# Two-layer graph network, 16 graphs: the turning of the first norm's output moves from TensorE to VectorE and DRAM

## The chip, the cores and the metric

The kernel runs on one core of one Trainium2 chip. What counts is the device time of one execution in microseconds (us), the median of the runs. A profiled execution gives a page of figures and a trace; its times are counted from its first instruction to its last (the span). Engines: PE is TensorE (matmuls), DVE is VectorE, ACT is ScalarE, POOL is GpSimd, and SP only issues transfers.

## The reference

The input is x, 16 graphs of 1024 nodes with 256 channels, and one matrix adj of 1024x1024. Everything is float32.

```python
# layer 0
h = jnp.maximum(_layernorm(x, axis=-1), 0.0)
c = mean of h over the channels                 # one number for each node
A = |sigmoid(c_m - c_n) - 0.5| ...              # weights from the differences
g = relu(einsum('bcn,bnm->bcm', h^T, adj * A_s) * para)   # becomes the queries q
k, v = split(h @ kv_w)
out = softmax(q k^T * scale) v                  # 4 heads of 64 channels
x = x + out
# layer 1
h = jnp.maximum(_layernorm(x, axis=-1), 0.0)
agg = A_hat @ h                                 # A_hat: adj + 1, normed by degrees
y = agg @ W1.T + b1;  batchnorm over all nodes of all graphs;  relu
z = h1 @ W2.T + b2;   batchnorm over all nodes of all graphs
x = x + z
```

The products `h @ kv_w` contract over the channels. A matmul on TensorE contracts over the partitions, so h, which lies with nodes in the partitions, must be turned: `ht` has channels in the partitions and nodes in the row. This turning is what the change concerns. Attention sums over all keys, so the order of the keys is free, as long as k and v have the same order.

## The kernel before

A graph's x lies as 8 tiles of 128 nodes, `[128, 8, 256]`. For each graph b the kernel makes: the first norm's output `h_a`; the weighed matrix tiles `w` (ScalarE: `Abs`, then `Tanh`; VectorE: times `adj`); the queries `q` (products `pg`); `ht`; keys and values (products `pk` and `pv`, from `ht`); attention; the second norm's output `h_b`; the aggregation (products `pa`, with tiles `aht` of the graph matrix kept in DRAM); and the hidden layer (products `py`, results `y` written to DRAM by POOL). When all graphs are through, a second part reads `y` back and ends the work.

The order is written out by hand. `attention()` walks through 16 steps for each graph: two score tiles `sc` (TensorE), their exponentials `p` (ScalarE, four buffers), the additions `acc` (VectorE), the products with the values `o` of the step before. Beside the attention of graph b, a generator `background(b)` supplies the other work in pieces: the remaining products for graph b+1 (keys, queries, values), the aggregation of graph b-1, and `prepare(b + 2, ...)` with the hidden products of graph b-1. Every piece has a cost (1.71 for a product) and the loop takes pieces until a share of `total` is reached, about three products in each step. A piece that yields `TOP` asks that the next piece stand behind the scores at the top of the next step.

`prepare(b, products)` issues one hidden product, three more with three slots of the weighing `w`, then the turning of one half of the channels at the top of a step, again products with weighing, the turning of the other half, and the rest. `transposed(b, k)` does the turning: for each of two halves of the nodes four TensorE transposes of 128x128 into one PSUM bank (`htp`, line 396), and one ScalarE copy of 128x512 from the bank to `ht` (line 399). The banks of all these products come from one pool, `ps_mm`, with two buffers, so a product can start only when the one two before it has been copied out.

Other pools that matter: tag `h` (two buffers, for `h_a` and `h_b`), tag `ht` (three buffers, shared by `ht` and the aggregation's result `at`), tag `adj` (three buffers). SP's queue holds the loads of `adj`, `para`, `aht` and `x` in the order in which they are issued; a load that must wait holds those behind it. POOL's queue holds the small steps of the norms and the writes of `y`, of x and, in graph 0, the work on the graph matrix (`graph()`).

Of the kernel before, what the change touches and what calls it, by code (L numbers as in the profile page):

```python
# [10 lines left out]
F32 = mybir.dt.float32  # L11
# [6 lines left out]
P = 128  # L18
# [5 lines left out]
def gnn_two_layers_kernel(  # L24
# [12 lines left out]
    nc = tc.nc  # L37
    B, N, C = x.shape
    H1 = w1_t.shape[1]
    NT = N // P  # L40
    CC = C // P
# [11 lines left out]
    dram = ctx.enter_context(tc.tile_pool(name="dram", bufs=1, space=DRAM))  # L53
# [15 lines left out]
    aht_d = dram.tile([7, NP // 2, P, TH, FB], F32, name="aht_d")  # L69
    y1_d = [dram.tile([P, HC, FB], F32, name=f"y1_d{i}") for i in range(B * NH)]  # L70

    csum_d = [dram.tile([N], F32, name=f"csum_d{b}") for b in range(B)]
    dinv_d = dram.tile([N], F32, name="dinv_d")

# [5 lines left out]
    SQ = 32  # L80
    NS = P // SQ
# [14 lines left out]
    def layers(shifted):  # L96
# [10 lines left out]
        p2 = st.enter_context(tc.tile_pool(name=f"p2_{kind}", bufs=2))  # L107
        p3 = st.enter_context(tc.tile_pool(name=f"p3_{kind}", bufs=3))
# [11 lines left out]
        xs, hs, hts, ats, qs, ks, vs = {}, {}, {}, {}, {}, {}, {}  # L120
        invs = {}
        csums, cbcs, weighted, weighers = {}, {}, {}, {}
# [9 lines left out]
        def advance(pieces):  # L132

            due = queue[:]
            queue.clear()
            cost = next(pieces, None)
            for action in due:
                action()
            return cost

        def run(*parts):
            for part in parts:
                while advance(part) is not None:
                    pass
            while queue:
                queue.pop(0)()

        def weave(main, *sides):

            for i, cost in enumerate(main):  # L150
                for start, side in sides:
                    if i >= start:
                        cost += next(side, 0.0)
                yield cost
            for _, side in sides:
                yield from side
# [7 lines left out]
        def bank(name):  # L164
            return ps_mm.tile([P, FB], F32, tag="mm", name=name)
# [217 lines left out]
        TOP = -1.0  # L383

        def transposed(b, k, halves=range(NH)):

            h = hs["a", b]
            if 0 in halves:
                ht = p3.tile([P, N], F32, tag="ht", name=f"ht_{b}_{k}")
                hts.setdefault(b, []).append(ht)  # L390
            ht = hts[b][k]
            for g in halves:
                pt = bank(f"htp_{b}_{k}_{g}")
                for j in range(FB // P):
                    t = g * (FB // P) + j
                    nc.tensor.transpose(
                        pt[:, j * P : (j + 1) * P], h[:, t, k * P : (k + 1) * P], ident
                    )
                nc.scalar.copy(ht[:, g * FB : (g + 1) * FB], pt)  # L399

        def differences(b):

            cbc = p1.tile([P, N], F32, tag="cbc", name=f"cbc_{b}")
            cbcs[b] = (
                cbc.rearrange("p (t q) -> p t q", t=NT)
                if b <= 1
                else cbc.rearrange("p (q t) -> p t q", t=NT)
            )  # L410
            weighers[b] = weigh(b)
            if b == 0:
                broadcast_row(cbc, columns_of(csums[b], f"c{b}"), f"c{b}")
                return
            if b == 1:
                turned = bank(f"csumt_{b}")[0:NT, 0:P]
                nc.tensor.transpose(turned, csums[b], ident)
                row = p1.tile([P, NT // 2, P], F32, tag="s1", name=f"csumr_{b}")[0:NT, 0, :]
                nc.scalar.copy(row, turned)
                nc.sync.dma_start(out=csum_d[b].rearrange("(t p) -> t p", p=P), in_=row)  # L420
            else:
                nc.sync.dma_start(out=csum_d[b].rearrange("(p t) -> p t", p=P), in_=csums[b])
            nc.sync.dma_start(
                out=cbc, in_=csum_d[b].rearrange("(o n) -> o n", o=1).to_broadcast([P, N])
            )
# [43 lines left out]
        AHEAD = 6  # L469
# [310 lines left out]
        def prepare(b, products):  # L780


            yield from islice(products, 1)
            w = weighers[b]
            for k in range(CC):
                yield from weave(islice(products, 3), (0, islice(w, AHEAD // 2)))
                yield TOP
                transposed(b, k)
                yield 1.0
            yield from products  # L790

        endings, turns = [], []
# [89 lines left out]
        def scores(b, k, f, g):  # L882


            made = []
            for m in (2 * g, 2 * g + 1):
                sc = ps_sc.tile([P, 2, FB], F32, tag="sc", name=f"sc_{b}_{k}_{f}_{m}")
                for e in range(2):
                    r = slice(e * HD, (e + 1) * HD)
                    nc.tensor.matmul(  # L890
                        sc[:, e, :],
                        ks[b][k][r, m * P : (m + 1) * P],
                        qs[b][k][r, f * FB : (f + 1) * FB],
                        start=True,
                        stop=True,
                    )
                pr = p4.tile([P, 2, FB], F32, tag="p", name=f"p_{b}_{k}_{f}_{m}")
                nc.scalar.activation(pr, sc, AF.Exp)  # L898
                made.append(pr)
            return made  # L900
# [107 lines left out]
        def attention():  # L1008

            units = [Unit(b, k, f) for b in range(B) for k in range(CC) for f in range(NH)]  # L1010
            steps = [(u, g) for u in units for g in range(NG)]
            per_graph = CC * NH * NG
            before = None
            at_top, at_end, adds = {}, {}, {}
            bg, done, total, top = iter(()), 0.0, 0.0, False
            for s in range(len(steps) + 2):
                if s < len(steps):
                    unit, g = steps[s]
                    b = unit.at[0]
                    if s % per_graph == 0:  # L1020
                        run(bg)
                        top = False
                        bg, done = background(b), 0.0
                        total = (37.6 if b > 0 else 41.0) * (b + 1 < B) + 24.0 * (b > 0) + 6.0 * (b + 2 < B)
                        total += 13.7 * (0 < b < B - 2) + 27.4 * (b == B - 1) + 3.0 * (b == 0)

                        total -= 10.3 * (b == B - 1)
                    made = scores(*unit.at, g)
                    due = total * (s % per_graph + 1) / per_graph
                else:  # L1030
                    due += 5.1
                for action in at_top.pop(s, ()):
                    action()
                if top:
                    done += advance(bg)
                    top = False
                if s in adds:
                    adds.pop(s)()
                if s < len(steps):
                    for pr in made:  # L1040
                        unit.add(pr)
                if before is not None:
                    (last, g_last), prs = before
                    last.values(g_last, prs)
                    if g_last == NG - 1:

                        one = (0, 0, 1, 1) if last.index == UNITS - 1 else (0, 1, 3, 4)
                        for e in range(2):
                            at_end.setdefault(s + one[e], []).append(lambda u=last, e=e: u.fold(e))
                        at_top.setdefault(s + one[2], []).append(last.sums)  # L1050
                        at_top.setdefault(s + one[3], []).append(last.finish)
                        adds[s + one[3]] = last.add_output
                while done < due and not top:
                    cost = advance(bg)
                    if cost is None:
                        break
                    if cost == TOP:
                        top = True
                        break
                    done += cost  # L1060
                for action in at_end.pop(s, ()):
                    action()
                before = (steps[s], made) if s < len(steps) else None
            run(bg)

        with st:
# [22 lines left out]
            else:  # L1089
# [10 lines left out]
                products = keys_values(0)  # L1100
# [9 lines left out]
                load_x(2)  # L1110
                run(weave(plain_queries(0), (0, weighers[0]), (5, Norm(1, True).all())))
                attention()
                attn.close()
                turns.append(second(kind))
# [325 lines left out]
```

## Time and profile before

| | us |
|---|---|
| median of 3 runs | 2608.92 |
| lowest and highest run | 2606.27, 2610.16 |
| span of the profiled execution (time around it is not listed) | 2604.3 |
| PE busy | 2525.9 |
| DVE busy | 1822.7 |
| ACT busy | 1460.7 |
| POOL busy | 391.3 |
| PE L396, `htp`, 256 transposes, busy (they overlap) | 36.5 |
| ACT L399, copies to `ht`, 64 | 34.6 |

Busy time of an engine says how long instructions ran on it, not that the kernel waited for it. The chain of work that ended last says for each moment of the span what the end waited for. In the timeline a row is a run of equal instructions: start, length, engine, line, operation, output from inputs, count, and in brackets the idle time before with what ended it. Matmuls overlap, so the distance between starts says more than the lengths.

### The profile page before, as it was taken

The numbers are of one execution on the slowest core, as the hardware profiler recorded it, in microseconds if no ns is written. First come the engines' busy times: TensorE is split into PE (matmuls) and PEld (weight loads), VectorE is DVE, ScalarE is ACT, GpSimd is POOL, SyncE is SP. The second block draws the span as 40 slices with busy tenths as digits, with TensorE's granted clock in tenths as the row PEclk, the third lists the DMA queues.
The fourth block names the chain that finished last, engine by engine and source line by source line (L and its number), as shares of the span: only waits on it lengthen the run. The fifth ranks groups of instructions, "written<-read, shape, count | busy, mean of one in ns | idle before, by whom it ended". The sixth has DMA issues, their size and how long they took to land.

```text
span 2604.3 us, 31375 instructions
## 1 busy us (share of the span) xinstructions
PE 2525.9 (97%) x11627; PEld 931.8 (36%) x11627; DVE 1822.7 (70%) x2837; ACT 1460.7 (56%) x2034; POOL 391.3 (15%) x456
## 2 busy tenths in 40 slices
PE   7999999999999999999999999999999999999994
PEld 3333333333333333333333333333333333334443
DVE  4768686867767686868677676858686776657774
ACT  6774565647474746656464747465564634335543
POOL 1540001000101000010001010000100001036653
PEclk9999999999999999999999999999999999999997
DMA  3654224152524343241525243433315242355459
GB/s 138 229 171 173 93 99 154 54 189 73 182 83 152 111 148 101 102 150 55 183 71 182 86 156 107 147 100 114 137 62 180 66 166 105 109 196 221 170 198 367
DMA packets 130915, 363.46 MB, mean 140 GB/s; under 512 B 15288, under 2 KB 32192, under 8 KB 124608
## 3 DMA queue, kind: packets, MB, share of 16 engines
q1 hardware_dynamic: 110144, 282.70, 31.3%
q0 software_dynamic: 20608, 78.66, 7.9%
q8 instruction: 94, 1.54, 0.2%
q14 instruction: 69, 0.57, 0.1%
HBM read 286.79 MB, written 74.51 MB: 139 GB/s over the span
## 4 chain that ended last, share of the span: by engine, by line
PE 87%; ACT 7%; DMA 2%; issue 2%; DVE 1%; SPq 0%; POOL 0%; POOLq 0%; DVEq 0%; ACTq 0%
PE sc L890 17%; PE o L931 16%; PE pa L171 15%; PE pg L171 14%; PE py L171 8%; PE m_f L1235 7%; PE pk L171 4%; PE pv L171 4%; ACT w L458 3%; DMA out_dram<-xo_f 2%; ACT p L898 2%; PE ot L986 1%; ACT w L466 1%; PE sums L961 1%; ACT ht L399 1%
## 5 line engine op out<-in xcount | busy, mean ns | idle before, releaser
L898 ACT ACTIVATE p<-sc 128x1024 f32<-128x1024 f32 x512 | 495.0, 1020 | 452.5 <-PE sc L890 452.1
L920 DVE TENSOR_TENSOR acc<-acc,p 128x1024 f32<-128x1024 f32 x384 | 472.2, 1230 | 143.2 <-ACT p L898 121.8
L890 PE MATMUL sc<-q,k 64*128 64x512 f32 x2048 | 509.0, 615 | 4.7 <-ACT p L898 4.6
L931 PE MATMUL o<-p,v 128*64 128x512 f32 x2048 | 495.9, 605 | 0.0
L171 PE MATMUL pg<-w,h_a 128*64 128x512 f32 x1600 | 357.9, 592 | 3.1 <-DVE q L612 2.3
L171 PE MATMUL pa<-aht,h_b 128*64 128x512 f32 x1536 | 344.0, 592 | 3.5 <-ACT h_b L341 3.4
L890 PEld LDWEIGHTS sc<-q,k 64*128 64x128 f32 x2048 | 175.9, 186 | 325.5 <-issue 284.4
L458 ACT ACTIVATE w<-cbc,csum 128x512 f32<-128x512 f32 x256 | 285.5, 1168 | 0.0
L171 PE MATMUL py<-at,w 128*64 128x512 f32 x1024 | 232.8, 597 | 8.4 <-ACT ht L399 7.0
L445 DVE SCALAR_TENSOR_TENSOR w<-w,adj 128x1024 f32<-128x1024 f32 x128 | 157.5, 1230 | 114.8 <-ACT w L466 110.8
L931 PEld LDWEIGHTS o<-p,v 128*64 128x64 f32 x2048 | 124.1, 136 | 250.3 <-issue 247.2
L171 PEld LDWEIGHTS pg<-w,h_a 128*64 128x64 f32 x1600 | 114.7, 137 | 232.0 <-issue 214.4
L746 POOL DMA_DIRECT2D y_d<-y x128 | 70.5, 551 | 795.0 <-ACT y L745 787.2
L171 PEld LDWEIGHTS pa<-aht,h_b 128*64 128x64 f32 x1536 | 110.8, 137 | 216.9 <-issue 208.3
L745 ACT ACTIVATE y<-py,vec 128x512 f32<-128x512 f32 x128 | 87.6, 684 | 142.3 <-PE py L171 119.7
L749 DVE BATCH_NORM_STATS2 stats<-y 128x6 f32<-128x512 f32 x128 | 85.7, 687 | 79.6 <-ACT y L745 79.5
L466 ACT ACTIVATE w<-w 128x1024 f32<-128x1024 f32 x128 | 135.2, 1056 | 1.7
L520 DVE TENSOR_TENSOR w<-w,w 128x1024 f32<-128x1024 f32 x112 | 132.8, 1217 | 1.5
L341 ACT ACTIVATE h_b<-x,lnsm_b 128x256 f32<-128x256 f32 x128 | 70.4, 609 | 110.7 <-DVE lnsm_b L330 110.7
L93 POOL TENSOR_SCALAR lnsm_b<-mv_b 128x4 f32<-128x4 f32 x32 | 12.1, 379 | 791.5 <-DVE mv_b L319 791.4
L171 PEld LDWEIGHTS py<-at,w 128*64 128x64 f32 x1024 | 72.2, 137 | 162.4 <-issue 129.8
L171 PE MATMUL pk<-ht,kvw_f 128*64 128x512 f32 x512 | 117.0, 599 | 1.5 <-ACT ht L399 1.5
(158 smaller groups left out, 2779.7 us busy)
## 6 DMA issues: line engine op xcount, KB each, us to landing
aht<-aht_d SPq DMA_DIRECT2D x224, 512.0 KB, 6.3
adj<-in_adj_dram SPq DMA_DIRECT2D x128, 512.0 KB, 4.4
y_d<-y POOLq DMA_DIRECT2D x128, 256.0 KB, 2.6
yin_f<-y_d SPq DMA_DIRECT2D x32, 1024.0 KB, 6.3
x<-in_x_dram SPq DMA_DIRECT2D x32, 512.0 KB, 5.1
para<-in_para_dram SPq DMA_DIRECT2D x64, 256.0 KB, 3.9
x_d<-x POOLq DMA_DIRECT2D x16, 1024.0 KB, 10.3
xo_f<-x_d SPq DMA_DIRECT2D x32, 512.0 KB, 8.6
```

Of the source, the lines that this page charges most:

```text
L171: nc.tensor.matmul(dst[r], left[:, r], right, start=start, stop=stop)
L445: nc.vector.scalar_tensor_tensor(w, w, 1.0, a, op0=ALU.add, op1=ALU.mult)
L458: nc.scalar.activation(w[:, t, :].rearrange("p (t q) -> p t q", q=P), cbc[:, q * NT // NH : (q + 1) * NT // NH], AF.Abs, bias=csum[:, th * ...
L466: nc.scalar.activation(made[i], made[i], AF.Tanh, scale=-0.5 / C)
L520: nc.vector.tensor_sub(block(i)[part], block(x)[part], block(y)[part])
L745: nc.scalar.activation(y, made, AF.Identity, bias=b1[:, j : j + 1])
L749: nc.vector.bn_stats(stats1[:, j, i, :], y)
L890: nc.tensor.matmul(sc[:, e, :], ks[b][k][r, m * P : (m + 1) * P], qs[b][k][r, f * FB : (f + 1) * FB], start=True, stop=True,)
L898: nc.scalar.activation(pr, sc, AF.Exp)
L920: nc.vector.tensor_add(self.acc, self.acc, pr)
L931: nc.tensor.matmul(self.o[r, :], vs[b][k][:, m, r], pr[:, e, :], start=(m == 0), stop=(m == NT - 1),)
L1235: nc.tensor.matmul(made, left[:, j, :], right[:, j, :], start=(j == 0), stop=(j == JH - 1))
```

## The change

From graph 2 on (`prepare` serves graphs 2 to 15; graphs 0 and 1 are still turned by TensorE) `transposed` is replaced by two functions. `squares(b)` lets VectorE transpose each square of 32x32 in place of the whole, for both halves of the channels, into a third tile of tag `h`, and POOL writes this tile, 1 MB, to a new DRAM tensor `hsq_d`. `gathered(b, k)` lets SP read it back into `ht`, in four transfers for each half of the channels: each fills 32 partitions with 4 runs of 256 elements from 4 groups of partitions. So the squares reach their places between partitions, and the nodes in `ht` stand in another order than before, the same for keys and values. In `prepare` the pieces are arranged anew: `squares` after the first hidden product, `gathered(b, 0)` after the fourth, `gathered(b, 1)` after the fifth; no piece asks for the top of a step. The cost of the turning in `total` becomes 4.0 for 6.0.

```diff
+    hsq_d = [dram.tile([P, CC, N], F32, name=f"hsq_d{b}") for b in range(B)]
...
+        def squares(b):
+            sq = p2.tile([P, CC, N], F32, tag="h", name=f"sq_{b}")
+            for k in range(CC):
+                nc.vector.transpose(
+                    sq[:, k].rearrange("p (i t s) -> p i t s", i=NS, s=SQ),
+                    hs["a", b][:, :, k * P : (k + 1) * P].rearrange("p t (i s) -> p i t s", s=SQ),
+                )
+            nc.gpsimd.dma_start(out=hsq_d[b], in_=sq)
+
+        def gathered(b, k):
+            ht = p3.tile([P, N], F32, tag="ht", name=f"ht_{b}_{k}")
+            hts.setdefault(b, []).append(ht)
+            src = hsq_d[b][:, k].rearrange("(j s) (i r) -> i s j r", s=SQ, i=NS)
+            for i in range(NS):
+                nc.sync.dma_start(
+                    out=ht[i * SQ : (i + 1) * SQ].rearrange("s (j r) -> s j r", j=NS), in_=src[i]
+                )
...
         def prepare(b, products):
+            w = weighers[b]
             yield from islice(products, 1)
-            w = weighers[b]
-            for k in range(CC):
-                yield from weave(islice(products, 3), (0, islice(w, AHEAD // 2)))
-                yield TOP
-                transposed(b, k)
-                yield 1.0
+            squares(b)
+            yield from weave(islice(products, 3), (0, islice(w, AHEAD // 2)))
+            gathered(b, 0)
+            yield from weave(islice(products, 1), (0, islice(w, 1)))
+            gathered(b, 1)
+            yield from weave(islice(products, 2), (0, islice(w, AHEAD // 2 - 1)))
             yield from products
...
-                        total = (37.6 if b > 0 else 41.0) * (b + 1 < B) + 24.0 * (b > 0) + 6.0 * (b + 2 < B)
+                        total = (37.6 if b > 0 else 41.0) * (b + 1 < B) + 24.0 * (b > 0) + 4.0 * (b + 2 < B)
```

## The prediction

> **What bounds the kernel now.** I read the page first (busy shares, then the chain of work that ended last), and then the timeline of TensorE around one set of the transposes that the change removes.
>
> ```profile
> PE 2525.9 (97%) x11627; PEld 931.8 (36%) x11627; DVE 1822.7 (70%) x2837; ACT 1460.7 (56%) x2034; POOL 391.3 (15%) x456
> ...
> PE 87%; ACT 7%; DMA 2%; issue 2%; DVE 1%; SPq 0%; POOL 0%; POOLq 0%; DVEq 0%; ACTq 0%
> ```
>
> TensorE is busy 97% of the span and holds 87% of the chain; VectorE, at 70%, holds 1%. So TensorE's order is the clock of the middle part. The pieces of the chain confirm it: the first product `pk` of a graph starts at these times.
>
> ```profile
> 321.76 5.15 PE pk L171 x24
> ...
> 464.61 5.15 PE pk L171 x24
> ...
> 607.46 5.15 PE pk L171 x24
> ```
>
> The distance is 142.85 us each time. A graph that takes exactly as long as the last one is set by one engine that doesn't wait for varying things. Hence time taken from TensorE inside such a period should come off the span, unless something new is late.
>
> Now the transposes of graph 5 (`htp`), in the timeline of TensorE (start, length, operation, count, idle time before):
>
> ```profile
> 724.49 1.94 PE L931 MATMUL o<-p,v 128*64 128x512 f32 x8
> 726.26 1.89 PE L171 MATMUL py<-at,w 128*64 128x512 f32 x8
> 728.08 1.99 PE L890 MATMUL sc<-q,k 64*128 64x512 f32 x8
> 729.99 1.09 PE L396 MATMUL htp<-ident,h_a 128*128 128x128 f32 x8
> 731.02 1.94 PE L931 MATMUL o<-p,v 128*64 128x512 f32 x8
> 733.50 5.37 PE L171 MATMUL py<-at,w 128*64 128x512 f32 x24 [0.54 <-ACT ht L399]
> 738.80 1.99 PE L890 MATMUL sc<-q,k 64*128 64x512 f32 x8
> 740.72 0.41 PE L961 MATMUL sums<-part,same 128*128 128x32 f32 x2
> 740.96 1.07 PE L396 MATMUL htp<-ident,h_a 128*128 128x128 f32 x8
> 741.96 1.94 PE L931 MATMUL o<-p,v 128*64 128x512 f32 x8
> 744.00 1.94 PE L171 MATMUL py<-at,w 128*64 128x512 f32 x8
> ```
>
> Read start to start, since matmuls overlap. The two groups of 8 take 1.03 and 1.00 us. After `o`, the next product normally starts 1.77 us later (724.49 to 726.26); after the first group it starts 2.48 us later and after the second 2.04 us, so 0.71 and 0.27 us more. That is `py` waiting for one of two PSUM banks until ScalarE has copied `htp` out (L399).
>
> [...] the fold's 128x512 transpose takes 699 ns and an ordinary 128x512 addition about 690. [...] SP waits for POOL's write; the trace has such waits (SP for `x_d`, 13 times, 117.8 us in all, 9.9 at most).
>
> **The change part by part.**
>
> Removed, for each of 14 graphs (2 to 15): 16 transposes, 2.03 us of TensorE, and the two late starts, 0.98 us. Sum 3.0 us; I take 2.95, since `sums` then has the slightly longer step to `o` seen elsewhere (0.33 for 0.24 us). Four ScalarE copies (2.4 us) also go; I count them at nothing, because ScalarE is idle 44% of the time.
>
> Added on VectorE: two transposes of 128x1024. By the 699 ns for half that width, and by the 1.23 us of other 128x1024 operations (about 1.15 start to start), some 2.4 us. Lower bound 2.3; upper bound, if runs of 32 elements cost double, 4.8. They stand behind the last addition and scaling of the aggregation, so at that point nothing new is waited for. Queued behind them are the statistics of `y`, the fold and the next `acc` additions, which free `p` for ScalarE. In 700 to 760 us VectorE has gaps of 1 to 4 us at every step, and the four `p` buffers leave about a step of 8.9 us. Taken at nothing; if that cover were gone, 2.4 us a graph.
>
> Added on POOL: one write of 1 MB, about 0.63 us of issue and 10.3 us to landing, by the `x_d` write of the same size (transfers to and from `x_d`: 3.9 to 13.7). Only the small `y_d` writes stand behind it: the second waits one issue longer, and its `y` buffer is wanted again four products later.
>
> Added on SP: 8 gathers of 128 KB in runs of 1 KB. SP needs about 0.45 us for an issue, so 3.6 us. Runs of 1 KB are known from the load of `x`: 512 KB land in 5.1 us. Two of these in a row, 10.2 us, bound 1 MB from above; 5.1 + 3.6 = 8.7 is what I take. Behind the gathers in SP's queue is the fourth load of `adj`, wanted only in the next graph (before, its use is at 756, some 25 us after it could be issued).
>
> **Is the trip hidden?** In the built program's order the hidden products `py` move together: two in one step of attention, three in each of the next two, and the last step has none. From the start of the first `py`, by the trace's distances (`sc` 1.92, `o` 1.77, a product 1.75, `ot` 0.59, `sums` 0.33 us): 3.5 + 8.94 + 8.94 + 4.02 + 4.28 = 29.7 us until the next graph's `pk`, which needs `ht`. The chain: final addition and scaling 1.4, transposes 2.4, write 10.3, gathers 8.7: 22.8 us. Spare, 6.9 us; with the slow ends (13.7 and 10.2) still 2. The transfer engines stand nearly still after 707 us, so no crowd is to be expected. Price when hidden: nothing.
>
> The empty step leaves ScalarE 4.0 us of TensorE time for two exponentials (first end 1.18 + 0.97 us after `sc` starts, second 3.1). Working through ScalarE's new order, the weighing before it ends in time by about 0.3 to 1 us. So no stall, but this is the thinnest place.
>
> Graph 0 is different (period 178.75 minus its start, with ScalarE and POOL as the limits). POOL's queue has the writing of the graph matrix and the `deg` power in front of the new write, and reaches them only at 164 to 167 us. Then a write of about 7 (10.3 was in a crowd of loads; bounds 5 and 10.3) and 8.7: `ht` of graph 2 lands near 183 where `pk` started at 178.75. That is a loss of about 4 us, bounds 0 and 8; the transposes' 2 us there were inside a ScalarE wait anyway (2.43 and 1.92 us of idle TensorE).
>
> **Sum.** 13 x 2.95 = 38.4 saved, 4 lost: 34.4 us. The profiled execution's span of 2604.3 becomes 2570; the page lists no time around the span, and the runs' median, 2608.92, stands 4.6 above it. So 2574.5.
>
> **Rivals.**
>
> A, the trip is late (ends slower). `pk` waits for the gathers, and as TensorE works in order everything behind it waits too. Each gather writes only 32 of 128 partitions, a shape that the trace before doesn't show. The point from which it decides: the trip longer than 29.7 us by more than the saving of 2.95, that is a write and gathers of about 29 us from issue to landing where I have 19. If eight gathers went at half the rate of `x` (20.4 us) behind a write of 13.7, the trip is 1.4 + 2.4 + 13.7 + 0.6 + 20.4 = 38.5, late by 8.8, net +5.9 in each of 13 graphs and some 16 in graph 0: about 2701. For it: the unknown shape. Against it: 16 transfer engines idle in that stretch, the spare 7 us. Chance 0.12.
>
> B, the saving is halved by a new wait. ScalarE or VectorE is late in the empty step (weighing, statistics and the transposes stand closer together), and `sc` waits for `p`; 1.5 us a graph: 38.4 - 19.5 - 4 = 15 us, 2594. For it: the waits of 2.43 and 1.92 us in graph 0, where weighing stood before an attention-only step. Against it: in the later graphs ScalarE waited only 0.3 us or more for work at these places and loses 2.4 us of copies. Chance 0.13.
>
> C, nothing moves: the freed TensorE time is all taken back as waits, or the transposes are overlapped by weight loads more than start-to-start shows. Against it: the 97% and the constant period. Chance 0.03.
>
> **How the numbers follow.** Main case 0.72: 2574.5, its own range 2566 (no loss in graph 0, 14 x 3.0 saved) to 2583. B reaches 2600. The range 2564 to 2600 takes in the main case and B with their bounds on the unknown costs and leaves A out, 0.12, and C, 0.03. Faster by over 0.2% (5.2 us, about what a measurement of this kernel can tell from no change): main case and B, 0.85; within: C, 0.03; slower: A, 0.12.
>
> **What would show it.** Right: no `htp` after graph 1; the first `pk` of neighbouring graphs 139.9 us apart; VectorE transposes of 128x1024 at 1.2 us; gathers landing several us ahead of `pk`; the waits of `py` for `ht` gone. Wrong: `pk` waiting for a DMA in each graph (A); `sc` waiting for `p` in the last step of a graph (B); transposes much above 1.2 us; a period that stays at 142.85 (C).

## The result, and the profile after

| | before | after |
|---|---|---|
| median, us | 2609.27 | 2572.42 |
| lowest and highest of 4 runs, us | 2606.27, 2610.16 | 2571.51, 2573.06 |
| span of the profiled execution, us | 2604.3 | 2570.6 |

The ratio is 0.986 (95% interval 0.9847 to 0.9872): faster by 36.9 us in the medians. The profiled execution after took 2572.44 us, 1.8 us more than its span, so its span stands for the median. The span of before does not: of the 29 executions of that kernel on record 7 took 2605.84 to 2606.69 us and 22 took 2608.5 to 2610.43, none lies between, and the profiled one, with a span of 2604.3, belongs to the 7.

The busy shares of the page after, to be held against those of before:

```profile
PE 2497.0 (97%) x11403; PEld 913.0 (36%) x11403; DVE 1851.1 (72%) x2865; ACT 1432.0 (56%) x1978; POOL 396.8 (15%) x470
```

TensorE has 224 matmuls and 28.9 us less. VectorE has 28.4 us more, ScalarE 28.7 us less, and TensorE is still the only engine near its limit.

The groups of instructions (line, engine, operation, output and inputs, shapes, count; busy time, mean ns of one; idle time of the engine before them and what ended it). First two lines: the transposes on TensorE and on VectorE. Third: the product that used to wait for ScalarE's copies. Last: the same product in the kernel before.

```profile
L397 PE MATMUL htp<-ident,h_a 128*128 128x128 f32 x32 | 6.2, 323 | 9.0 <-ACT h_a L342 8.5
...
L408 DVE STREAM_TRANSPOSE sq<-h_a 128x1024 f32<-128x1024 f32 x28 | 33.1, 1219 | 0.0
...
L172 PE MATMUL py<-at,w 128*64 128x512 f32 x1024 | 230.7, 598 | 0.0
...
L171 PE MATMUL py<-at,w 128*64 128x512 f32 x1024 | 232.8, 597 | 8.4 <-ACT ht L399 7.0
```

`htp` is left for two graphs only. The idle time in front of `py`, 8.4 us before, is 0.0.

The timeline of TensorE at the same place as before, the end of graph 5's preparation:

```profile
715.91 1.94 PE L955 MATMUL o<-p,v 128*64 128x512 f32 x8
717.68 5.32 PE L172 MATMUL py<-at,w 128*64 128x512 f32 x24
722.93 1.99 PE L914 MATMUL sc<-q,k 64*128 64x512 f32 x8
724.85 1.94 PE L955 MATMUL o<-p,v 128*64 128x512 f32 x8
726.62 5.32 PE L172 MATMUL py<-at,w 128*64 128x512 f32 x24
731.87 1.99 PE L914 MATMUL sc<-q,k 64*128 64x512 f32 x8
...
740.26 5.32 PE L172 MATMUL pk<-ht,kvw_f 128*64 128x512 f32 x24
...
1998.79 5.32 PE L172 MATMUL pk<-ht,kvw_f 128*64 128x512 f32 x24
```

No row here has a bracket: TensorE waits for nothing. Every `o` to `py` is the ordinary 1.77 us. This `pk` and the one of the last graph, nine graphs later, are 1258.53 us apart (740.26 to 1998.79), so the period is 139.84 us, 3.01 less than before. The kernel before had its `pk` for graph 2 and for the last graph at these times:

```profile
178.75 5.32 PE L171 MATMUL pk<-ht,kvw_f 128*64 128x512 f32 x24
...
2035.77 5.32 PE L171 MATMUL pk<-ht,kvw_f 128*64 128x512 f32 x24
```

The changed kernel starts the first of them at 180.91, 2.2 us later, and the last 37.0 us earlier. Thirteen periods lie between the two: 13 x 3.01 = 39.1 us saved, 2.2 lost in graph 0.

The trip that replaces the transposes, from the timelines of VectorE, POOL and SP:

```profile
712.02 2.36 DVE L408 STREAM_TRANSPOSE sq<-h_a 128x1024 f32<-128x1024 f32 x2
```
```profile
714.68 0.54 POOL L412 DMA_DIRECT2D hsq_d<-sq  x1 [0.66 <-DVE sq L408]
```
```profile
718.97 4.21 SPq L420 DMA_DIRECT2D ht<-hsq_d  x8
```

The write is issued at 714.68 and SP's gathers follow at 718.97, 4.3 us later. The eight issues end at 723.18; with a median of 4.0 us from issue to landing (2.4 to 6.3 over all 112 gathers) the last one is there at about 727. `pk` needs it at 740.26: some 13 us to spare.

### The profile page after: what moved, and what is told of

Its sections match the earlier page's. It is cut to its first block, busy times and chain, and to the rows that moved or that the text cites. A ratio compares the mean times of both kernels' runs of the same rounds, so it can differ in the third digit from the quotient of the medians.

```text
span 2570.6 us, 31151 instructions
## 1 busy us (share of the span) xinstructions
PE 2497.0 (97%) x11403; PEld 913.0 (36%) x11403; DVE 1851.1 (72%) x2865; ACT 1432.0 (56%) x1978; POOL 396.8 (15%) x470
## 3 DMA queue, kind: packets, MB, share of 16 engines
q1 hardware_dynamic: 126272, 297.39, 33.7%
## 5 line engine op out<-in xcount | busy, mean ns | idle before, releaser
L172 PE MATMUL pk<-ht,kvw_f 128*64 128x512 f32 x512 | 117.9, 603 | 1.5 <-ACT ht L400 1.5
L172 PE MATMUL pv<-kvw_f,ht 128*64 128x256 f32 x1024 | 115.9, 379 | 0.0
## 6 DMA issues: line engine op xcount, KB each, us to landing
x_d<-x POOLq DMA_DIRECT2D x16, 1024.0 KB, 10.3
```

The source lines that it names most:

```text
L172: nc.tensor.matmul(dst[r], left[:, r], right, start=start, stop=stop)
```

## The experiments

The theory: the transposes' TensorE time and the late starts behind them are the saving; the trip through DRAM is hidden; 2.2 us were lost in graph 0; and between the two profiled executions another 3.3 us were lost in the end part. The main rival is that the new arrangement of `prepare`, not the turning, moved the time. All ratios are to the kernel before on the same chip.

### The arrangement alone

```diff
-            squares(b)
...
-            gathered(b, 0)
+            transposed(b, 0)
...
-            gathered(b, 1)
+            transposed(b, 1)
```

> The change's arrangement of the hidden products and its smaller total are kept, but the turning is done by TensorE as before (16 transposes and 4 ScalarE copies a graph, at the places of the gathers, not at the top of a step). Theory (the saving is TensorE's own time, 2.03 us of transposes and 0.98 us of waiting for PSUM banks a graph): the period returns from 139.84 to between 141.9 (transposes alone) and 142.85 us, the time to 2598 to 2611. Rival (the new arrangement of the pieces made the gain): the period stays near 139.9 and the time near 2572.

Measured: 2658.32 us (2658.27 to 2660.06), ratio 1.019 (1.0173 to 1.0207). The direction was as expected, the size was a miss: 49 us slower than before, where at most the old time was expected. TensorE's timeline shows why:

```profile
740.59 0.66 PE L397 MATMUL htp<-ident,h_a 128*128 128x128 f32 x4
741.45 0.66 PE L397 MATMUL htp<-ident,h_a 128*128 128x128 f32 x4 [0.20 <-ACT y L768]
744.15 2.68 PE L172 MATMUL py<-at,w 128*64 128x512 f32 x8 [2.04 <-ACT ht L400]
746.75 2.90 PE L913 MATMUL sc<-q,k 64*128 64x512 f32 x8
```

and ScalarE's in the same stretch:

```profile
740.71 0.69 ACT L768 ACTIVATE y<-py,vec 128x512 f32<-128x512 f32 x1
741.29 2.33 ACT L481 ACTIVATE w<-cbc,csum 128x512 f32<-128x512 f32 x2
743.53 1.05 ACT L400 COPY ht<-htp 128x512 f32<-128x512 f32 x2
```

Away from the top of a step, the transposes follow directly on products, and the copies that must empty their banks stand behind a `y` and 2.33 us of weighing. `py` waits 2.04 us, and after it TensorE runs two groups slowly (`sc` 2.83 us from start to start, where 1.92 is usual). Neighbouring `pk` are 146.68 us apart (766.48 to 913.16), 3.8 more than before: 13 x 3.8 = 49 us. So the arrangement is not the source of the gain: with the old turning in it, it loses. Other places for the transposes in it were not tried.

### The transposes put back, without copies

At the top of two steps of each of 14 graphs (each one step earlier than the old ones), on constant data that nobody reads:

```diff
+                if s < len(steps) and b < B - 2 and s % per_graph in (13, 14):
+                    pt = bank(f"again_{s}")
+                    for j in range(8):
+                        r = slice(j % 4 * P, j % 4 * P + P)
+                        nc.tensor.transpose(pt[:, r], kvw[:, j % 2, r], ident)
```

> The changed kernel with 16 transposes of 128x128 put back on TensorE in each of 14 graphs, of constant data, read by nobody (no copy, no wait of a product for one): 8 behind the scores of the 14th and 8 behind those of the 15th step, where the old ones stood. Theory (two thirds of the saving is TensorE time of the transposes, one third the waits for the copies): 13 x 2.03 = 26.4 us come back and in graph 0 0 to 2 more, so 2597 to 2602 us, period 141.9 us, spare of the trip through DRAM longer by 2 us. Rival 1 (the waits for ScalarE's copies were the bulk, the transposes themselves cost little beside weight loads): under 2590 us. Rival 2 (ScalarE gains from the added 2 us, or TensorE's clock falls with the added work): over 2605 us or under 2590 us.

Measured: 2598.48 us (2597.9 to 2600.04), ratio 0.9964 (0.995 to 0.9977), 26.1 us above the changed kernel. The timeline of TensorE:

```profile
722.79 1.09 PE L1060 MATMUL again<-ident,kvw_f 128*128 128x128 f32 x8
723.81 1.94 PE L955 MATMUL o<-p,v 128*64 128x512 f32 x8
725.58 5.32 PE L172 MATMUL py<-at,w 128*64 128x512 f32 x24
...
749.18 5.32 PE L172 MATMUL pk<-ht,kvw_f 128*64 128x512 f32 x24
...
2026.16 5.32 PE L172 MATMUL pk<-ht,kvw_f 128*64 128x512 f32 x24
```

The eight cost 1.02 us, and `py` follows `o` after 1.77 us, with no late start. The period, from this `pk` to the one nine graphs on at 2026.16, is 141.89 us: 2.05 more than after, 0.96 less than before. That splits the saving of 3.01: two thirds is TensorE's own time. The other third is what is left, and it fits the 0.98 us by which `py` started late behind the copies in the kernel before; no run has the copies alone. Both rivals fell.

### The trip made longer

VectorE transposes everything twice, and POOL makes three writes of 1 MB, the last of them read back.

```diff
-            for k in range(CC):
+            for k in (0, 1, 0, 1):
...
+            for i in range(2):
+                nc.gpsimd.dma_start(out=hsq_e[i][b], in_=sq)
             nc.gpsimd.dma_start(out=hsq_d[b], in_=sq)
```

> As the change, but VectorE transposes every square twice (2.4 us more a graph) and POOL writes the tile three times (two writes of 1 MB into other DRAM tensors ahead of the one that is read), so the trip is some 11 us longer. Theory (the trip is hidden, with about 13 us to spare between the last gather and the first pk, and VectorE has cover): 2572 to 2576. Rival 1 (VectorE's 2.4 us are paid in part): about 1 us or more a graph, 2587 or more. Rival 2 (the trip is on the path or close to it): several us a graph, 2620 or more.

Measured: 2576.36 us (2574.33 to 2577.94), ratio 0.9871 (0.9855 to 0.9888), 0.4 above the expected range. The trip grew by less than the expected 11 us, and `pk` still waits for nothing. SP, then TensorE:

```profile
728.81 5.94 SPq L425 DMA_DIRECT2D ht<-hsq_d  x8
```
```profile
742.65 5.32 PE L175 MATMUL pk<-ht,kvw_f 128*64 128x512 f32 x24
```

The next graph's `pk` is at 882.49: a period of 139.84 us, the changed kernel's. Counted back from `pk`, the gathers start 7.4 us later than in the changed kernel (13.8 us ahead of it for 21.3) and their issue ends 9.2 us later (7.9 us ahead for 17.1). Twice the VectorE work and this delay are both hidden here. The profiled execution is the longest of the four, its span 5.5 us above that of the changed kernel. Of these, 2.4 are already in this `pk` (742.65 for 740.26) and come from graph 0, where the trip has no spare:

```profile
184.11 4.51 PE L175 MATMUL pk<-ht,kvw_f 128*64 128x512 f32 x20 [1.31 <-DMA ht<-hsq_d]
```

Another 2.0 us arose in a single later period (141.88 us, from 1721.84 to 1863.72), for a wait of 1.8 us of `py` for ScalarE's `y` that the groups show. No later `pk` waits for the trip.

### The trip started too late

From graph 3 on, `squares` comes after the fifth hidden product and both `gathered` after the seventh, two steps later than in the change.

```diff
-            squares(b)
-            yield from weave(islice(products, 3), (0, islice(w, AHEAD // 2)))
+            if b == 2:
+                squares(b)
+            yield from weave(islice(products, 4), (0, islice(w, 4)))
+            if b > 2:
+                squares(b)
+            yield from weave(islice(products, 2), (0, islice(w, 2)))
             gathered(b, 0)
```

> As the change, but from graph 3 on the squares are made after the fifth hidden product instead of the first, and the gathers after the seventh. By the trace of the change VectorE then gets to the squares some 17 us later, which is more than the 13 us to spare: the last gather should land about 4 us after the time at which pk could start. Theory: pk waits for the gathers 4 us in each of 13 graphs, period about 144, time about 2625 (2600 to 2650), slower than the kernel before. Rival (something else, such as the weighed matrix, sets the start of pk, or TensorE makes the wait good later): under 2585.

Measured: 2628.96 us (2624.07 to 2629.48), ratio 1.007 (1.0054 to 1.0087): slower than before. The group of `pk`, and two of its rows in the timeline of TensorE:

```profile
L172 PE MATMUL pk<-ht,kvw_f 128*64 128x512 f32 x512 | 134.2, 662 | 40.4 <-DMA ht<-hsq_d 38.9 <-ACT ht L400 1.5
```
```profile
756.11 1.08 PE L172 MATMUL pk<-ht,kvw_f 128*64 128x512 f32 x4 [1.24 <-DMA ht<-hsq_d]
759.91 5.39 PE L172 MATMUL pk<-ht,kvw_f 128*64 128x512 f32 x12 [2.72 <-DMA ht<-hsq_d]
```

Waits of 38.9 us, and 16.3 us more of busy time (134.2 for 117.9: behind the wait at 759.91 twelve matmuls take 5.39 us, where 24 usually take 5.32), make 55.2 of the 56.5 us lost against the changed kernel. This is the prediction's rival A, made real: its mechanism exists, and what decides is the distance between write and use.

### Graph 0: the weighing spread out

Only for graph 2, prepared beside graph 0's attention, the six slots of weighing are divided over several steps, with the gathers between them:

```diff
+            if b == 2:
+                squares(b)
+                yield from weave(islice(products, 1), (0, islice(w, 1)))
+                for i in range(5):
+                    next(w)
+                    if i in (1, 2):
+                        gathered(b, i - 1)
+                    yield 1.0
+                return
```

> As the change, but for graph 2 alone, which is turned in graph 0, the six slots of weighing are spread over the last three steps of attention instead of standing together in one. Theory (in graph 0 the 2.2 us that were lost came from ScalarE's weighing in one lump, after which the scores waited 5.2 us for an exponential and ran slowly for one group, and not from the trip through DRAM): the first pk for graph 2 starts 2 to 5 us earlier than at 180.9, time 2567.5 to 2570.5. Rival (the trip of graph 2 sets that start, POOL being late): pk waits for the gathers and starts at about the same time, 2572.

Measured: 2569.73 us (2565.74 to 2571.26), ratio 0.9846 (0.9829 to 0.9862). TensorE in the changed kernel, and then here:

```profile
174.95 3.68 PE L914 MATMUL sc<-q,k 64*128 64x512 f32 x8 [5.17 <-ACT p L922]
...
180.91 5.32 PE L172 MATMUL pk<-ht,kvw_f 128*64 128x512 f32 x24
```
```profile
170.71 2.04 PE L923 MATMUL sc<-q,k 64*128 64x512 f32 x8 [0.78 <-ACT p L931]
...
176.49 1.08 PE L172 MATMUL pk<-ht,kvw_f 128*64 128x512 f32 x4 [1.28 <-DMA ht<-hsq_d]
178.98 5.99 PE L172 MATMUL pk<-ht,kvw_f 128*64 128x512 f32 x20 [1.41 <-DMA ht<-hsq_d]
```

In the change all six slots of weighing fall into one step of graph 0, so ScalarE is late with `p`, and `sc` waits 5.17 us and then runs slowly. Spread out, that is gone, `pk` starts 4.4 us earlier, and now it does wait for the trip (1.28 + 1.41 us). The weighing was the limit in graph 0, with the trip close behind it. The gain of 2.7 us is about half of what the prediction takes to be clear of noise. The trace carries 1.3 us of it: the `pk` four graphs on is at 738.99 for 740.26, and the last one is as much earlier (1997.52 for 1998.79). What the profiled execution gained beyond that, 1.9 us, arose in the end part, which this edit does not touch, and the next experiment shows where.

### The idle gaps of the end part filled

In the two profiled executions it is 571.8 us from the last `pk` to the end after and 568.5 before (1998.79 and 2035.77 to the end of the span), though TensorE's order there is the same. Two groups differ, behind gaps that both kernels have. TensorE after:

```profile
2161.39 3.55 PE L172 MATMUL pa<-aht,h_b 128*64 128x512 f32 x8 [2.74 <-ACT h_b L342]
...
2243.35 0.53 PE L985 MATMUL sums<-part,same 128*128 128x32 f32 x2 [4.98 <-DVE part L973]
...
2245.21 7.89 PE L172 MATMUL py<-at,w 128*64 128x512 f32 x24
```

and before:

```profile
2198.37 1.94 PE L171 MATMUL pa<-aht,h_b 128*64 128x512 f32 x8 [2.74 <-ACT h_b L341]
...
2278.66 0.63 PE L961 MATMUL sums<-part,same 128*128 128x32 f32 x2 [4.96 <-DVE part L949]
...
2280.62 6.43 PE L171 MATMUL py<-at,w 128*64 128x512 f32 x24
```

The first differs by 1.61 us and the second by 1.46, together 3.1 of the 3.3 us; smaller differences further on have both signs. The granted clock says the same: 0.76 at 2159 to 2164 after, 1.00 at 2196 to 2201 before. To see whether idleness is the cause, dummy products fill both gaps:

```diff
+        def fill(n, name):
+            made = bank(f"fill_{name}")
+            for i in range(n):
+                e = i % 2
+                nc.tensor.matmul(
+                    made[e * HW : (e + 1) * HW],
+                    kvw[:, 0, e * HW : (e + 1) * HW], kvw[:, 1, :], start=True, stop=True,
+                )
...
+                if b == B - 1:
+                    fill(12, "h")
...
+                        if last.index == UNITS - 1:
+                            at_top.setdefault(s + one[2], []).append(lambda: fill(22, "f"))
```

> The changed kernel with dummy products of constant data in two places of the end part, ahead of the first aggregation of graph 15 (12 matmuls, into the idle gap of 2.74 us) and ahead of the last sums (22 matmuls, into the gap of 4.98 us), so that TensorE isn't idle there. Theory (TensorE runs slower for a few us after an idle gap, 1.61 us lost behind the first and 1.46 us or more behind the second, which is what the span lost in the end part): the time from the last graph's first key product to the end falls from 571.8 us to 568 to 570 us, and the time from 2572.4 to 2569 to 2571 us. Rival (the slow groups have nothing to do with idle time, or the dummies stand in the way): 571 us or more to the end, time 2572 us or more.

Measured: 2575.07 us (2574.3 to 2575.47), ratio 0.9871 (0.9856 to 0.9886): a miss. With the spread weighing as well:

> The changed kernel with both amendments: the weighing for graph 2 spread over several steps in graph 0 (which alone gave 2569.7 us) and the two idle gaps of TensorE in the end part filled with dummy products. Theory: the two add up, 2566 to 2568.5 us. Rival (the slow clock after idle is not removed by filling): 2569 us or more.

Measured: 2573.5 us (2572.36 to 2574.66), ratio 0.9865 (0.985 to 0.988), a miss too. The timeline of the first one shows a mistake of size:

```profile
2159.38 5.32 PE L822 MATMUL fill_h<-kvw_f 128*64 128x512 f32 x24
2164.53 1.89 PE L172 MATMUL pa<-aht,h_b 128*64 128x512 f32 x8
```

Each dummy shows as two matmuls, so the fills took 5.15 and 9.54 us for gaps of 2.9 and 5.15 from end of work to start of work. The slow groups themselves were gone (`pa` 1.81 us from start to start for 3.48, `py` 5.20 for 7.72). Half the number, 6 and 11, was the repair:

> As the filled version, but with half as many dummy products (6 and 11, each of which shows as two matmuls of 0.215 us), 2.6 and 4.7 us for gaps of 2.9 and 5.15 us; the long fills had taken away the slow groups (first aggregation 1.81 us for 3.48, the last hidden products 5.20 for 7.72) but were 2.2 and 4.4 us longer than the gaps. Theory (slow only because of the idle time before): about 1.7 and 3.1 us less than the changed kernel's 2572.4, so 2567 to 2568.5 us, both groups at their usual speed. Rival (the gaps' remainders of 0.3 us, or the dummies' own bank, cost it back, or the slow spell only moves elsewhere): 2571 us or more.

Measured: 2568.84 us (2567.69 to 2569.0), ratio 0.985 (0.9836 to 0.9863), 3.6 us below the changed kernel and 0.3 above the expected range.

```profile
2159.00 2.75 PE L822 MATMUL fill_h<-kvw_f 128*64 128x512 f32 x12
2161.92 1.94 PE L172 MATMUL pa<-aht,h_b 128*64 128x512 f32 x8 [0.17 <-ACT h_b L342]
```

The same work at the same distance from the same `h_b`, without the idle time, runs at its usual speed: 1.86 us from start to start, for 3.48 in the changed kernel. The part from the last `pk` (1999.32) to the end is 567.5 us. The traces of all the kernels show both places (time of the group from its start to the next group's start):

| profiled execution | first aggregation, `pa`, us | last hidden products, `py`, us |
|---|---|---|
| before | 1.87 | 6.26 |
| after | 3.48 | 7.72 |
| arrangement alone | 3.27 | 7.43 |
| transposes put back | 1.87 | 7.42 |
| longer trip | 3.25 | 7.43 |
| late trip | 3.14 | 6.14 |
| weighing spread out | 1.87 | 7.50 |
| gaps filled (four kernels) | 1.81 to 1.86 | 5.20 to 5.21 |

Without the fills the gaps are equally long everywhere (2.74 to 2.75 and 4.96 to 4.98 us), and the loss comes and goes; with them it is gone each time. So the lost time does follow the idle time, but it is not a cost of the change: the kernels with the weighing spread out and with the transposes put back have the changed end part too, and lose nothing at the first gap. Nor is it needed between the medians: they fell by 36.9 us, as much as 39.1 - 2.2, and the profiled execution of before is one of its short ones. Whether its longer executions lose their 3 us at these gaps is not shown; there is no trace of one. And both amendments together:

> The short fills together with the weighing for graph 2 spread in graph 0. Theory: both savings add, 2564 to 2566.5 us. Rival (they don't add): 2567.5 us or more.

Measured: 2565.03 us (2562.84 to 2569.91), ratio 0.9838 (0.9825 to 0.9851), the shortest median of all and in the expected range. Its executions spread over 7 us, so that the two savings add in full is likely, but not sharply shown.

## Why the prediction was right, point by point

The forecast was 2574.5, the result 2572.42, and the mechanism was the one described. Its steps:

- **TensorE as the clock; 2.95 us a graph.** Held: 3.01 measured as a period, and divided into 2.05 for the transposes put back and 0.96 for the rest, where the working had 2.03 and 0.98 (rounded down for `sums`). Over 13 periods 39.1 us, not 38.4.
- **VectorE's transposes at 1.2 us, hidden.** Held: 1219 ns each, two in 2.36 us; doubled, they left the period at 139.84 us.
- **The trip.** It was hidden, but mis-sized, on the safe side. The write took 4.3 us (4.2 to 5.3), not 10.3: the `x_d` row that priced it is a median in a crowd of other transfers (the `x_d` write issued at 1075.61 in the changed kernel took 10.7 us with 2.6 MB of `aht` loads beside it), and this place is quiet, with only writes of `y_d` beside it. The transfer engines fell still at about 711 us in the kernel before (busy 92% from 707 to 711 us, 0% from there to 720), not 707, which did no harm, since the write starts at 714.68. The gathers took about 8.2 us from the first issue to the last landing, for 8.7. From the first `py` to `pk` it was 29.8 us for 29.7. Spare: some 13 us, not 6.9. The gathers' shape, each filling 32 partitions, had no row before; 4.0 us for each is its price here.
- **The empty step.** Held, and as thin as said: in graph 5 its exponentials end at 735.41 and the scores behind them start at 735.99, 1.87 us after `o` for the usual 1.77.
- **Graph 0.** The size was 2.2 us, not 4 (`pk` 180.91 for 178.75), within the bounds of 0 to 8, but the cause given was wrong, so that the size came near was luck. The step that failed is the reading that POOL's late write would set the end there. SP issued the gathers at 171.0 to 175.0 already, since the write was short. What set it was ScalarE's lump of weighing, a wait for `p` that the prediction listed under rival B for the later graphs. With that removed, the trip becomes the limit.
- **The sum.** 39.1 - 2.2 = 36.9 us, which is what the medians fell by. The forecast had 38.4 - 4 = 34.4 and so was 2.5 us too careful: 0.7 in the periods and 1.8 in graph 0, both on the same side. The spans of the two profiled executions fell by only 33.7. That this lies close to 34.4 is chance: 3.3 us went in the end part, behind idle gaps that the prediction did not look at and whose cost comes and goes.
- **The time around the span.** The 4.6 us added to reach the median were not time around the span: every execution on record whose span is listed takes 1.8 to 2.1 us more than it. A span of 2604.3 thus belongs to a time of about 2606.3, that of the lowest run (2606.27), and the rest of the 4.6 is the distance from this execution to the median. It did no harm, because the saving was in effect taken off the median of before.
- **The rivals.** A did not occur; started later it costs 56 us, and 7 to 9 us of delay still cost nothing in the steady graphs. B's wait occurred in graph 0 alone. C fell: the transposes put back cost what they had cost before.

## What to carry to other kernels

Where one engine's period is constant, its start-to-start distances price a removed operation well, waits for its copies included (here 2.95 us a graph, and 3.01 measured); put the operation back as a dummy to see how the saving divides. Before a difference between two profiled executions is put down to a change, see where each stands among the other executions of its kernel. A transfer's median comes with the traffic around its row (1 MB took 4.3 us in a quiet place and 10.7 us beside 2.6 MB of loads), so price a trip by the rows of its own surroundings, and what decides is the work between its start and its use. Look also at the ends of the loop, where a steady gain meets lumps of other engines' work, and at TensorE's idle gaps: here one of 2.74 us cost up to 1.6 us beyond its own length.

## What was not expected of the hardware

TensorE ran slowly behind an idle gap, and not behind every one: by the table above, a gap of 2.74 us cost 1.3 to 1.6 us in four profiled executions and nothing in three, and the one of 4.98 us cost 0.9 to 2.5 us in all seven. The granted clock shows it too. Behind the first gap it was 0.53 in the changed kernel (2161.39 to 2164.87) and 1.00 in the kernel before (2198.37 to 2200.24); in the gap itself it was 1.00 in both. Behind the second, during `py`, it was 0.67 in the changed kernel (2245.21 to 2252.93) and 0.83 in the kernel before (2280.62 to 2286.90). There the mean over the gap was already 0.73 (2273.70 to 2278.66), where it was 1.00 in the changed kernel (2238.37 to 2243.35). So the clock did not fall at the same point of the same work. Why a gap of one length costs time in one execution and not in another was not settled; that it was the idle time was, by filling both gaps: with the longer fills the granted clock was 1.00 from 2156 to 2174 and from 2230 to 2262.
